# A stated order for TensorE: one attention layer of a later group at four fixed places of every gated step

## The chip, the cores and the metric

The kernel runs on one core of one Trainium2 chip. A core has TensorE (PE in the profile: matrix products and transposes, results in eight PSUM banks), VectorE (DVE), ScalarE (ACT), GpSimd (POOL), and SyncE (SP), whose queue issues the transfers. The metric is the device time of one execution in microseconds (us). Before the change it is 3129.03 us, the median of three runs (3125.44 to 3129.26).

## What is computed

128 graphs of 128 nodes with 256 features go through three attention layers and then a gated recurrent network of three steps. All is float32. Cut to what matters:

```python
# three attention layers, l = 0, 1, 2
h  = relu(layernorm(x))
Wh = h @ W                                    # per graph [128, 256]
e  = (Wh @ a1)[:, None] + (Wh @ a2)[None, :]  # [128, 128]
e  = where(e > 0, e, 0.2 * e)
p  = softmax(where(adj > 0, e, -9e15), axis=-1)
x  = x + elu(p @ Wh)                          # layer 2: (p @ Wh) * nodemask

# gated network, i = 0, 1, 2
h  = relu(layernorm(x))
for i in range(3):
    aggr = A.T @ (h @ weight[i])              # A = (adj != 0)
    r = sigmoid(aggr @ w_ih_r.T + b + h @ w_hh_r.T + b)
    z = sigmoid(aggr @ w_ih_z.T + b + h @ w_hh_z.T + b)
    n = tanh(aggr @ w_ih_n.T + b + r * (h @ w_hh_n.T + b))
    h = (1 - z) * n + z * h
x = x + h
```

The kernel computes `attention @ h` before the product with `W`, reads `Wh @ a1` and `Wh @ a2` as products of h with the vectors `W a1` and `W a2` (`VA`), and folds `weight[i]` into `w_ih` once at the start (`wc[i]`). The sigmoids are taken as tanh of half the argument.

## The kernel before

Graphs are worked on in 32 groups of four (G = 4, T = 512 columns). `gat(g)` is the three attention layers of a group, `gru(g)` its gated steps. PSUM has three pools of banks: "gat" 2, "gru" 4, "tr" 2. One layer:

```python
def attention(g, l, xt, cap):
    nm, rs = stats(xt, name)        # VectorE bn_stats/bn_aggr; GpSimd: rs = (var + eps) ** -0.5
    for b in range(G):              # ScalarE
        nc.scalar.activation(xn[:, b, :], xt[:, b, :], AF.Relu, bias=nm[:, b : b + 1])
    for b in range(G):              # VectorE: e[:, 0] = xn . VA[0]
        nc.vector.scalar_tensor_tensor(scr, xn[:, b, :], rs[...], VA[l][:, 0, :], ..., accum_out=e[:, 0, b : b + 1])
    nc.gpsimd.tensor_tensor(pr, xn, VA[l][:, 1 : 2, :]..., op=OP.mult)       # GpSimd
    for b in range(G):              # ScalarE: e[:, 1] = sum of pr
        nc.scalar.activation(pr[:, b, :], pr[:, b, :], AF.Copy, scale=rs[...], accum_out=e[:, 1, b : b + 1])
    yield
    for c in range(G):              # TensorE, "e" in the profile
        nc.tensor.transpose(e2[...], e[:, 1, c : c + 1].to_broadcast([P, P]), ident)
    # ... VectorE: em = min(e2 + e[:, 0], cap), leaky relu, row maximum nmx
    # ... ScalarE: pe = exp(em - max), sums;  VectorE: pe *= 1 / sum
    # ... GpSimd: xo = xt - 1
    yield
    for b in range(G):              # TensorE, "atp"
        nc.tensor.transpose(atp[...], pe[:, b, :], ident)
    # ... VectorE: at = atp * rs
    # ... TensorE "ahp": 2 x 4 products 128x128; copies ah by ScalarE and VectorE
    # ... TensorE "hp": 2 x 4 products 128x256; ScalarE t = exp(hp); VectorE: two xo per half
    yield xo
```

After the third layer the normalised features `hn` are turned by TensorE for the gated steps (`hTp`: eight transposes of 128x128, one copy on ScalarE, one on VectorE):

```python
hT = turned(hn, grp, "h0", f"{g}_3")
```

A gated step has 24 products of 128x512, eight of 128x128 (`agp`) and, from the second step on, eight transposes (`hnp`):

```python
for i in range(STEPS):
    for c in range(KD):                       # KD = 2
        nn, pr, pz = ...                      # three "gru" banks
        if c == 0: evac(0)                    # hnp transposes of h[0], ScalarE copy (not for i == 0)
        for k in range(KD):
            mm(nn, cn, whh, h, k, ...); mm(pr, cr, whh, h, k, ...); mm(pz, cz, whh, h, k, ...)
            if c == 0:
                aggregate(k)                  # agp: 4 products, VectorE copy ag[k]
                if k == 0: evac(1)
        # ScalarE: wn
        yield
        # TensorE r <- ag (k = 0, 1); ScalarE r = tanh; VectorE n = (r + 1) * wn
        # TensorE ni <- ag (k = 0, 1); VectorE n += ni; ScalarE n = tanh
        yield
        # TensorE z <- ag (k = 0, 1); ScalarE z = tanh
        # VectorE d = h[c] - n;  d = (z + 1) * d;  hnew[c] = 0.5 * d + n
        yield
# end: for k in 0, 1: hnp transposes of h[k]; VectorE o = hnp + xt; transfer out
```

The program emits whole streams, group after group:

```python
AHEAD = 2
for g in range(min(AHEAD, NG)):
    run(gat(g))
for g in range(NG):
    run(gru(g))
    if g + AHEAD < NG:
        run(gat(g + AHEAD))
```

What stands next to what on an engine is thus left to the scheduler of the language, which reorders the instructions of every engine by a model of their times when the program is built.

Of the kernel before, what the change touches and what calls it, by code (L numbers as in the profile page):

```python
# [8 lines left out]
FT = mybir.dt.float32  # L9
# [5 lines left out]
P = 128  # L15
# [6 lines left out]
def kernel(  # L22
# [23 lines left out]

    nc = tc.nc
# [3 lines left out]
    NG = B // G  # L51
    T = G * N
    STEPS = gweight.shape[0]
    assert N == P and B % G == 0 and B <= P and D == 2 * P and T == 512

    const = ctx.enter_context(tc.tile_pool(name="const", bufs=1))
    grp = ctx.enter_context(tc.tile_pool(name="grp", bufs=2))
    gw = ctx.enter_context(tc.tile_pool(name="gw", bufs=2))
    setup = ExitStack()
# [6 lines left out]

    def load(g):
        xt = grp.tile([P, G, D], FT, tag="x0", name=f"x_{g}")
        nc.sync.dma_start(xt, x[g * G : (g + 1) * G].rearrange("b n d -> n b d"))
        at = grp.tile([P, G, N], I32, tag="adj", name=f"adj_{g}")  # L70
        nc.sync.dma_start(at, adj[g * G : (g + 1) * G].rearrange("b i j -> i b j"))
        return xt, at

    loaded = {0: load(0)}


# [38 lines left out]

    def transposed(src, dst, nm_):
# [3 lines left out]
        for k in range(KD):  # L120
            for r0 in range(0, rows, 4):
                n = min(4, rows - r0)
                ps = bank("gat", f"{nm_}_{k}_{r0}")
                for r in range(n):
                    nc.tensor.transpose(
                        ps[:, r * P : (r + 1) * P], t[:, r0 + r, k * P : (k + 1) * P], ident
                    )
                nc.vector.tensor_copy(dst[:, k, r0 * P : (r0 + n) * P], ps[:, : n * P])
# [11 lines left out]
    for i in range(STEPS):  # L140
# [3 lines left out]
        for m in range(KD):  # L144
            for o0 in range(0, O3, 384):
                ps = bank("gat", f"wcp_{i}_{m}_{o0}")
# [18 lines left out]

    setup.close()
# [3 lines left out]
    def stats(xt, name):  # L170

        st = gw.tile([P, G, 6], FT, tag="st", name=f"st_{name}")
        mv = gw.tile([P, G, 2], FT, tag="mv", name=f"mv_{name}")
        for b in range(G):
            nc.vector.bn_stats(st[:, b, :], xt[:, b, :])  # L175
            nc.vector.bn_aggr(mv[:, b, :], st[:, b, :])  # L176
        nm = gw.tile([P, G], FT, tag="nm", name=f"nm_{name}")
        nc.vector.tensor_scalar(nm, mv[:, :, 0], -1.0, None, op0=OP.mult)
        ve = gw.tile([P, G], FT, tag="ve", name=f"ve_{name}")
        nc.gpsimd.tensor_scalar(ve, mv[:, :, 1], EPS, None, op0=OP.add)  # L180
        rs = gw.tile([P, G], FT, tag="rs", name=f"rs_{name}")
        nc.gpsimd.tensor_tensor(rs, ve, mhalf, op=OP.pow)  # L182
        return nm, rs

    def turned(v, pool, tag, name):

        hT = pool.tile([P, KD, T], FT, tag=tag, name=f"hT_{name}")
        for k in range(KD):
            ps = bank("gat", f"hTp_{name}_{k}")
            for b in range(G):  # L190
                nc.tensor.transpose(
                    ps[:, b * P : (b + 1) * P], v[:, b, k * P : (k + 1) * P], ident
                )
            if k % 2 == 0:
                nc.scalar.copy(hT[:, k, :], ps)
            else:
                nc.vector.tensor_copy(hT[:, k, :], ps)
        return hT

    def attention(g, l, xt, cap):  # L200

        name = f"{g}_{l}"
        nm, rs = stats(xt, name)

        xn = gw.tile([P, G, D], FT, tag="xn", name=f"xn_{name}")
        for b in range(G):
            nc.scalar.activation(xn[:, b, :], xt[:, b, :], AF.Relu, bias=nm[:, b : b + 1])  # L207

        e = gw.tile([P, 2, G], FT, tag="e", name=f"e_{name}")
        for b in range(G):  # L210
            scr = gw.tile([P, D], FT, tag="scr", name=f"scr_{name}_{b}")
            nc.vector.scalar_tensor_tensor(  # L212
                scr, xn[:, b, :], rs[:, b : b + 1], VA[l][:, 0, :], op0=OP.mult, op1=OP.mult,
                accum_out=e[:, 0, b : b + 1],
            )
        pr = gw.tile([P, G, D], FT, tag="pr", name=f"pr_{name}")
        nc.gpsimd.tensor_tensor(  # L217
            pr, xn, VA[l][:, 1 : 2, :].to_broadcast([P, G, D]), op=OP.mult
        )
        for b in range(G):  # L220
            nc.scalar.activation(  # L221
                pr[:, b, :], pr[:, b, :], AF.Copy, scale=rs[:, b : b + 1],
                accum_out=e[:, 1, b : b + 1],
            )
        yield

        e2 = bank("gat", f"e2_{name}")
        for c in range(G):
            nc.tensor.transpose(  # L229
                e2[:, c * P : (c + 1) * P], e[:, 1, c : c + 1].to_broadcast([P, P]), ident  # L230
            )

        em = gw.tile([P, G, N], FT, tag="em", name=f"em_{name}")
        for c in range(G):
            nc.vector.scalar_tensor_tensor(
                em[:, c, :], e2[:, c * P : (c + 1) * P], e[:, 0, c : c + 1], cap[:, c, :],
                op0=OP.add, op1=OP.min,
            )
        nc.vector.scalar_tensor_tensor(em, em, ALPHA, em, op0=OP.mult, op1=OP.max)
        nmx = gw.tile([P, G], FT, tag="nmx", name=f"nmx_{name}")  # L240
        nc.vector.tensor_reduce(nmx, em, axis=AX.X, op=OP.max, negate=True)  # L241
        pe = gw.tile([P, G, N], FT, tag="pe", name=f"pe_{name}")
        sm = gw.tile([P, G], FT, tag="sm", name=f"sm_{name}")
        for b in range(G):
            nc.scalar.activation(  # L245
                pe[:, b, :], em[:, b, :], AF.Exp, bias=nmx[:, b : b + 1], accum_out=sm[:, b : b + 1]
            )
        ri = gw.tile([P, G], FT, tag="ri", name=f"ri_{name}")
        nc.vector.reciprocal(ri, sm)
        if l == 2:  # L250
            nc.vector.tensor_mul(ri, ri, nmT[:, g * G : (g + 1) * G])
        nc.vector.tensor_tensor(
            pe, pe, ri.rearrange("p (g o) -> p g o", o=1).to_broadcast([P, G, N]), op=OP.mult
        )

        xo = grp.tile([P, G, D], FT, tag=f"x{l + 1}", name=f"xo_{name}", bufs=3 if l == 2 else 2)
        nc.gpsimd.tensor_scalar(xo, xt, 1.0, -1.0, op0=OP.mult, op1=OP.add)  # L257
        yield
        atp = bank("gat", f"atp_{name}")
        for b in range(G):  # L260
            nc.tensor.transpose(atp[:, b * P : (b + 1) * P], pe[:, b, :], ident)  # L261
        at = gw.tile([P, T], FT, tag="at", name=f"at_{name}")
        nc.vector.tensor_tensor(
            at.rearrange("p (g i) -> p g i", g=G), atp.rearrange("p (g i) -> p g i", g=G),
            rs.rearrange("p (g o) -> p g o", o=1).to_broadcast([P, G, N]), op=OP.mult,
        )

# [27 lines left out]
        yield xo  # L295

    done = {}

    def gat(g):
        xt, adj_t = loaded.pop(g)  # L300
        if g + 1 < NG:
# [168 lines left out]
```

## Time and profile before

| engine | busy us | share of the span |
|---|---|---|
| TensorE, products and transposes | 2941.1 | 94% |
| TensorE, weight loads (beside them) | 1714.3 | 55% |
| VectorE | 2163.8 | 69% |
| ScalarE | 1349.4 | 43% |
| GpSimd | 530.0 | 17% |

The span of the profiled execution is 3125.1 us. TensorE works in the first 50 us on setup (transposing and folding the weights), then on the first attention layers, and gated steps begin at 121 us. From 200 us on the picture repeats from group to group. A float32 product shows as two matmul records in the trace, a transpose as one. [...] the time of a product is read from the distance between starts. "Idle before" in brackets at the end of a timeline row is how long the engine had nothing running, and the arrow names what ended that.

### The profile page before, as it was taken

The page shows a single profiled execution, that of the slowest core. Times are in us where ns is not written, and L with a number is a line of the kernel's source. Part 1 is how long each engine was busy: PE and PEld are TensorE (multiplying, and loading weights), DVE is VectorE, ACT ScalarE, POOL GpSimd, SP SyncE. Part 2 cuts the span into 40 slices and gives each one's busy share as a digit, 9 for nine tenths or more (in the row PEclk, how much of TensorE's full clock was granted, in tenths as well). Part 3 has the DMA queues.
Part 4 walks back from the last instruction along what each step waited for, and adds up shares of the span by engine and source line. Part 5 has one row for each costly group of instructions (what it writes and reads, how often), then busy time and mean ns, then how long its engine had stood idle before and what let it go on. Part 6 is the DMA issues. An engine that isn't in the chain of part 4 may idle for free.

```text
span 3125.1 us, 32601 instructions
## 1 busy us (share of the span) xinstructions
PE 2941.1 (94%) x11105; PEld 1714.3 (55%) x11105; DVE 2163.8 (69%) x4731; ACT 1349.4 (43%) x3265; POOL 530.0 (17%) x454
## 2 busy tenths in 40 slices
PE   5699999999999999999999999999999999999999
PEld 3455555555555555555555555555555555555554
DVE  5667776767776777776777677677667677767663
ACT  1344444444444444444444444444444444444442
POOL 1212111212111212121112121112121121111110
PEclk8899999999999999999999999999999999999999
DMA  2000000000000000000000000000000000000000
GB/s 85 11 17 11 7 18 17 17 18 11 7 18 17 18 17 11 7 17 18 17 18 11 7 17 18 18 12 13 11 18 17 17 11 7 17 14 7 8 1 14
DMA packets 56199, 48.03 MB, mean 15 GB/s; under 512 B 3296, under 2 KB 55648, under 8 KB 56032
## 3 DMA queue, kind: packets, MB, share of 16 engines
q1 hardware_dynamic: 56032, 45.95, 4.6%
q8 instruction: 87, 1.43, 0.2%
q14 instruction: 80, 0.66, 0.1%
HBM read 29.17 MB, written 16.78 MB: 15 GB/s over the span
## 4 chain that ended last, share of the span: by engine, by line
PE 70%; DVE 13%; ACT 9%; POOL 6%; issue 1%; DMA 0%; ACTq 0%; SPq 0%; POOLq 0%; DVEq 0%
PE r L344 15%; PE z L344 15%; PE ni L344 9%; PE hp L285 7%; PE nn L344 7%; PE ahp L272 6%; POOL pr L217 5%; ACT xn L207 4%; PE agp L361 3%; DVE st L175 3%; DVE xo L294 3%; DVE xo L293 3%; ACT pr L221 2%; PE hnp L335 2%; PE e L229 2%; PE atp L261 2%
## 5 line engine op out<-in xcount | busy, mean ns | idle before, releaser
L212 DVE SCALAR_TENSOR_TENSOR scr<-xn,rs,va 128x256 f32<-128x256 f32 x384 | 386.0, 1053 | 73.0 <-POOL rs L182 71.1
L344 PE MATMUL r<-ag,wc 128*128 128x512 f32 x768 | 372.1, 593 | 0.0
L344 PE MATMUL ni<-ag,wc 128*128 128x512 f32 x768 | 371.4, 592 | 0.0
L285 PE MATMUL hp<-w,ah 128*128 128x256 f32 x1536 | 368.3, 383 | 0.7 <-DVE ah L279 0.7
L344 PE MATMUL z<-ag,wc 128*128 128x512 f32 x768 | 361.4, 592 | 0.0
L257 POOL TENSOR_SCALAR xo<-xo 128x1024 f32<-128x1024 f32 x64 | 67.5, 1055 | 1596.4 <-DVE mv L176 1596.4
L285 PEld LDWEIGHTS hp<-w,ah 128*128 128x128 f32 x1536 | 284.2, 190 | 76.8 <-DVE ah L279 26.3
L293 DVE SCALAR_TENSOR_TENSOR xo<-hp,xo 128x512 f32<-128x512 f32 x192 | 131.0, 683 | 253.6 <-ACT t L291 253.6
L221 ACT ACTIVATE pr<-pr,rs 128x256 f32<-128x256 f32 x384 | 190.4, 496 | 183.5 <-POOL pr L217 183.5
L291 ACT ACTIVATE t<-hp 128x512 f32<-128x512 f32 x192 | 114.7, 597 | 353.5 <-PE hp L285 353.5
L344 PE MATMUL nn<-h,whh 128*128 128x512 f32 x512 | 261.8, 593 | 0.0
L344 PE MATMUL z<-h,whh 128*128 128x512 f32 x512 | 261.5, 592 | 0.0
L344 PE MATMUL r<-h,whh 128*128 128x512 f32 x512 | 261.5, 592 | 0.0
L392 DVE SCALAR_TENSOR_TENSOR n<-r,wn 128x512 f32<-128x512 f32 x192 | 131.4, 685 | 185.2 <-ACT r L390 185.2
L217 POOL TENSOR_TENSOR pr<-xn,va 128x1024 f32<-128x1024 f32 x96 | 236.2, 2461 | 96.6 <-ACT xn L207 96.6
L245 ACT ACTIVATE pe<-em,nmx 128x128 f32<-128x128 f32 x384 | 148.8, 389 | 209.3 <-DVE nmx L241 209.3
L361 PEld LDWEIGHTS agp<-am,hn 128*128 128x128 f32 x1536 | 204.5, 192 | 61.3 <-issue 61.0
L344 PEld LDWEIGHTS z<-ag,wc 128*128 128x128 f32 x768 | 143.3, 190 | 167.5 <-issue 167.4
L397 ACT ACTIVATE n<-n,bi 128x512 f32<-128x512 f32 x192 | 138.3, 720 | 213.1 <-DVE n L396 210.5
L390 ACT ACTIVATE r<-r,brz 128x512 f32<-128x512 f32 x192 | 131.3, 684 | 215.1 <-PE r L344 215.0
L344 PEld LDWEIGHTS ni<-ag,wc 128*128 128x128 f32 x768 | 143.5, 190 | 142.7 <-issue 132.2
L361 PE MATMUL agp<-am,hn 128*128 128x128 f32 x1536 | 218.2, 275 | 0.0
(91 smaller groups left out, 4636.6 us busy)
## 6 DMA issues: line engine op xcount, KB each, us to landing
x<-in_x_dram SPq DMA_DIRECT2D x32, 512.0 KB, 3.9
out_dram<-o SPq DMA_DIRECT2D x32, 512.0 KB, 2.9
adj<-in_adj_dram SPq DMA_DIRECT2D x32, 256.0 KB, 2.7
w<-in_L_gnn_W_dram SPq DMA_DIRECT2D x3, 256.0 KB, 6.9
ab<-in_L_gnn_a_dram SPq DMA_DIRECT2D x3, 256.0 KB, 6.6
whh_ld<-in_L_gnn_w_hh_dram SPq DMA_DIRECT2D x1, 768.0 KB, 8.4
wih_ld<-in_L_gnn_w_ih_dram SPq DMA_DIRECT2D x1, 768.0 KB, 5.9
gt_ld<-in_L_gnn_weight_dram SPq DMA_DIRECT2D x3, 256.0 KB, 2.6
```

Source lines behind the costliest of these rows:

```text
L212: nc.vector.scalar_tensor_tensor(scr, xn[:, b, :], rs[:, b : b + 1], VA[l][:, 0, :], op0=OP.mult, op1=OP.mult, accum_out=e[:, 0, b : b + 1],)
L217: nc.gpsimd.tensor_tensor(pr, xn, VA[l][:, 1 : 2, :].to_broadcast([P, G, D]), op=OP.mult)
L221: nc.scalar.activation(pr[:, b, :], pr[:, b, :], AF.Copy, scale=rs[:, b : b + 1], accum_out=e[:, 1, b : b + 1],)
L245: nc.scalar.activation(pe[:, b, :], em[:, b, :], AF.Exp, bias=nmx[:, b : b + 1], accum_out=sm[:, b : b + 1])
L272: nc.tensor.matmul(ps[:, c * P : (c + 1) * P], xn[:, c, k * P : (k + 1) * P], at[:, c * P : (c + 1) * P], start=True, stop=True,)
L285: nc.tensor.matmul(hp[:, b * D : (b + 1) * D], ah[:, k, c * P : (c + 1) * P], W[l][:, k, :], start=(k == 0), stop=(k == KD - 1),)
L293: nc.vector.scalar_tensor_tensor(u, hp, 0.0, u, op0=OP.max, op1=OP.add)
L344: nc.tensor.matmul(ps, w[:, k, c * P : (c + 1) * P], v[k], start=start, stop=stop)
L361: nc.tensor.matmul(ps[:, b * P : (b + 1) * P], hn[k][b], am[:, b, :], start=True, stop=True)
L390: nc.scalar.activation(r, pr, AF.Tanh, bias=brz[:, cr : cr + 1], scale=0.5)
L392: nc.vector.scalar_tensor_tensor(n, r, 1.0, wn, op0=OP.add, op1=OP.mult)
L397: nc.scalar.activation(n, n, AF.Tanh, bias=bi[:, cn : cn + 1])
```

## The change

The change states TensorE's order in the program and alters what is needed for it. All other engines are still ordered by the scheduler. What it does:

- `manual_schedule` for TensorE around the main loop: its instructions stay as the program emits them. The gated steps are emitted with a raised priority for the other engines.
- Every gated step has four places. At each, one piece of an attention layer of a later group is emitted: e, then atp, then the ah products, then the hp products (with the next layer's statistics, xn, scr and pr). Step 0 of group g carries layer 2 of group g+1, step 1 layer 1 of group g+2, step 2 layer 0 of group g+3. The first statistics of group g+3 are emitted at the end of step 1.
- The groups are 2, then 31 times 4, then 2 graphs, so that the first chain and the last group are shorter.
- hTp is gone: VectorE transposes 32x32 blocks, and a round trip through device memory (one transfer out, four in) puts the blocks in place. Step 0 reads h with a strided view.
- The setup of the gated weights is emitted among the first attention layers; inputs are loaded two groups ahead.

It is for a TensorE that always has a product ready: gated products between the pieces give the other engines time to prepare the next piece. The core of the diff, cut:

```diff
+    SIZES = [2] + [G] * ((B - 4) // G) + [2]
+    URGENT = 300
 ...
-        hT = turned(hn, grp, "h0", f"{g}_3")
+            nc.vector.transpose(
+                tr.rearrange("p j (k b c) -> p k b j c", k=KD, b=n)[:, k],
+                hn[:, :, k * P : (k + 1) * P].rearrange("p b (j r) -> p b j r", j=Q),
+            )
+        nc.sync.dma_start(d.rearrange("q r j f -> (q r) j f"), tr)
+        for j in range(Q):
+            nc.sync.dma_start(
+                hT[j * 32 : (j + 1) * 32], d[:, :, j, :].rearrange("q r f -> r q f")
+            )
 ...          # gru, one step: the four places are the yields
+                    if c == 0:
+                        aggregate(k)
+                        if k == 0:
+                            yield
+                            evac(1)
 ...
+            evac(0)
+            for c in range(KD):
+                wn, pr, pz = yield from h_parts(c)     # nn, r, z of h; agp; wn
+                if c == 1:
+                    yield
+                # r <- ag; r = tanh; n
+                if c == 1:
+                    yield
+                # ni <- ag; n; z <- ag; z = tanh; d; h
+                if c == 0:
+                    yield
 ...
-    for g in range(NG):
-        run(gru(g))
-        if g + AHEAD < NG:
-            run(gat(g + AHEAD))
+    with tc.manual_schedule(engines={mybir.EngineType.PE}):
+        for g in range(NG):
+            work = gru(g)
+            for i in range(STEPS):
+                for p in range(4):
+                    with tc.high_priority(offset=URGENT):
+                        next(work)
+                    piece(g + 1 + i)
+                if i == 1:
+                    piece(g + 3)
+            with tc.high_priority(offset=URGENT):
+                next(work)
```

Two details matter for the order. The ni and z products of the second half (c = 1) come after the fourth place, so they are emitted with the next step's first part. And after step 2 they are followed at once by the group's last transposes and its output, then by the next group's step 0.

## The prediction

> **What bounds the kernel now.** I read the page first (busy shares, slices), then TensorE's list of waits, then the timeline of one middle group.
>
> ```profile
> PE 2941.1 (94%) x11105; PEld 1714.3 (55%) x11105; DVE 2163.8 (69%) x4731; ACT 1349.4 (43%) x3265; POOL 530.0 (17%) x454
> ...
> PEclk8899999999999999999999999999999999999999
> ```
>
> ```profile
> PE e L229 <- ACT pr L221: 102.4, 125, 8.4
> PE hTp L191 <- ACT hn L317: 29.1, 33, 6.1
> PE atp L261 <- DVE pe L252: 16.6, 3, 5.8
> ```
>
> TensorE is busy 94% of the time and its clock is granted in full from the third of the forty slices on. The waits are few: total us, count, longest. The work itself can be counted. In the timeline a 512-column product is two rows of one matmul and starts 0.86 us after the one before; a 128x256 one takes 0.43, a 128x128 one 0.22, a transpose 0.108. One group of four graphs needs 72 x 0.858 = 61.8 (gated steps), 24 x 0.22 = 5.3 (aggregation), 24 x 0.22 = 5.3 and 24 x 0.43 = 10.3 (attention), 48 transposes = 5.2 and 8 more for hTp = 0.9: 88.8 us. In the trace the same place of two groups is 94.27 us apart (hp at 231.56, 325.82, 420.10 in the chain). So about 5.5 us of each group are gaps, most of them the wait of e for pr. The start adds to that: the first gated product runs at 121 us, and TensorE is busy only 51 of the first 100 us.
>
> The second thing to read is how long a layer's row of engines takes from its last product (hp, ending at 1554.15) to the next layer's e:
>
> ```profile
> 1554.15 1.02 PE L344 MATMUL ni<-ag,wc 128*128 128x512 f32 x2
> ...
> 1554.35 0.60 ACT L291 ACTIVATE t<-hp 128x512 f32<-128x512 f32 x1 [1.13 <-PE hp L285]
> ...
> 1556.04 0.67 DVE L294 SCALAR_TENSOR_TENSOR xo<-t,xo 128x512 f32<-128x512 f32 x1
> ...
> 1559.12 1.71 ACT L207 ACTIVATE xn<-xo,nm 128x256 f32<-128x256 f32 x4 [0.84 <-DVE nm L178]
> ...
> 1560.90 2.45 POOL L217 TENSOR_TENSOR pr<-xn,va 128x1024 f32<-128x1024 f32 x1 [0.28 <-ACT xn L207]
> ...
> 1561.07 2.56 DVE L212 SCALAR_TENSOR_TENSOR scr<-xn,rs,va 128x256 f32<-128x256 f32 x1
> ...
> 1563.39 0.51 ACT L221 ACTIVATE pr<-pr,rs 128x256 f32<-128x256 f32 x1 [1.99 <-POOL pr L217]
> ...
> 1564.04 0.32 PE L229 MATMUL e<-ident,e 128*128 128x128 f32 x1 [1.14 <-ACT pr L221]
> ```
>
> Columns: start, length, engine, line, what. From hp's end to xn 4.97 us, from xn to ACT's pr 4.27, the four pr with their accumulator reads 2.08 (until 1565.47): 11.3 us. This chain is the quantity the change plays with.
>
> [...] the scr row above takes 2.56 us beside pr instead of its median 0.482. [...]
>
> ```profile
> 118.28 2.17 PE L191 MATMUL hTp<-ident,hn 128*128 128x128 f32 x8 [6.05 <-ACT hn L317]
> 120.24 1.06 PE L361 MATMUL agp<-am,hn 128*128 128x128 f32 x4
> 121.09 1.18 PE L344 MATMUL nn<-hT,whh 128*128 128x512 f32 x2
> ```
>
> After 6.05 us idle the eight transposes take 1.96 us start to start instead of 0.87, the next row 0.85 instead of 0.44: about 1.7 us lost in all. [...]
>
> **The change, part by part.**
>
> 1. hTp goes: 0.9 us of TensorE per group, about 28 in all, with two copies. In come two block transposes on VectorE (estimate 0.6 to 0.7 each, as its other one-pass 128x512 operations of 0.68) and five transfers. Those are issued two gated steps (about 60 us) before they are needed, against 2 to 4 us each: hidden.
>
> 2. Group sizes 2, 4 x 31, 2. The same columns in all. The first chain before the gated steps is half as wide and no longer shares the start with a whole second group. I estimate gated steps from about 80 us (before: 121).
>
> 3. The order. TensorE's order in a middle group is now fixed, and the instruction order of the changed kernel, which can be read without running it, shows what the others do. In step 2 of each group TensorE comes to e of layer 0 of group g+3. Between that and the hp of step 1 (layer 1 of group g+2) lie only ni and z (4 x 0.858 = 3.43), hnp 0.43, three products 2.57 and agp 0.89: 7.3 us. ScalarE's order there, in 29 of the 33 groups, is:
>
> ```
> z_1_1  hn_2_0  xn_2 x4  pr_2 x4  xn_0 x4  pr_0 x4  hn_2_1
> ```
>
> xn_2 and pr_2 belong to the layer that follows that hp, xn_0 and pr_0 to layer 0, which TensorE waits for. So the chain above runs first, then a second one behind it. Counted from hp's end: xn_2 starts at 4.97 plus what VectorE's order now puts in front (d 0.6 and the first x statistics 0.4) = 6.0; pr_2 done on ScalarE at 6.0 + 4.3 + 2.1 = 12.4; [...] then come the rest of the x statistics, so xn_0 starts at about 12.6; pr_0 is done at 12.6 + 4.3 + 2.1 = 19.0, e at 19.3. Without a wait e would end at 7.3 + 0.43 = 7.75. **Wait: 11.5 us in each of 29 groups.** It is long enough to halve the clock: 2.0 more.
>
> 4. The group's end. hnp of the second half of h now follows the last z with only the first hnp (0.43) between. The end of the kernel before shows what that costs:
>
> ```profile
> 3117.01 0.60 PE L335 MATMUL hnp<-ident,h 128*128 128x128 f32 x4
> ...
> 3118.97 0.69 DVE L408 SCALAR_TENSOR_TENSOR h<-d,n 128x512 f32<-128x512 f32 x1
> ...
> 3119.81 0.63 PE L335 MATMUL hnp<-ident,h 128*128 128x128 f32 x4 [2.19 <-DVE h L408]
> ```
>
> 2.19 us there with VectorE free; with hp's xo and statistics in VectorE's queue I count 2.7, in every group. Before, the next group's products stood in this gap.
>
> 5. r takes ag of the second half 0.86 us after agp ends; the copy needs 0.68 and VectorE's queue has reduce or em in front: 0.3 to 0.5 per step, estimate 0.9 per group (in step 2 hidden behind the cold clock). The other places hold: atp is needed 9 us after e, its chain takes 5 to 6; ah 5 us after atp, needs 0.7; hnp in a step 4.3 us after z, needs 2.3.
>
> **Sum.** A middle group: 88.0 + 11.5 + 2.0 + 2.7 + 0.9 = 105.1 us (before 94.27). Start 80. First group of two graphs, with three whole layers between its short steps: 35 + 18.3 of work and about 27 of waits (e of layer 0 alone 15.5) = 80. Middle groups 29 x 105.1 = 3048. Group 30 has no layer 0 beside it, group 31 only half a layer: 83 and 76. Last group of two and the output: 46. Together 80 + 80 + 3048 + 83 + 76 + 46 = 3413. I predict **3410 us**, 9% slower.
>
> **Rivals.** A: the stated order does what it is for. All waits fall: 32 x 88.0 = 2816, start 80, end 15, about 2910. For it speak the room between a layer's other places and the long slack of layers 1 and 2 (a step and more). Against it speaks the count of part 3: two chains of 6.4 us behind one of 6.0 do not fit into 7.3. B: ScalarE has room (43% busy) and layer 0's xn is done before the other layer's pr, so e waits only 3 to 5 us and the clock stays up: 88 + 4 + 3.6 = 95.6 per group, total near 3130, no change. The order read from the program speaks against it[...]. C: VectorE (67 of 94 us busy before) becomes the bound: it would need 88 us of work per group and has about 68; it only delays.
>
> **Range and chances.** The wait of part 3 is certain in sign; its size is the sum of about ten rows and may be off by 2 us (60 in all), the clock by 1.5 per group (45), the start by 25. Range 3300 to 3490. Faster by over 2%: 0.04 (A, if I read a dependence wrongly). Within 2%: 0.04 (B). Slower: 0.92.
>
> **What would show it.** TensorE's waits would be led by e for ScalarE's pr: some 30 times 11 us, 330 in all, in step 2 only; hnp for h about 2.7 x 33 = 85; TensorE's busy share near 85%; granted clock below full in every slice. The same place of two groups would be 105 us apart; gated steps begin near 80. Wrong if e's wait is under 5 us, if the clock stays full, or if the strided operand of step 0 (blocks of 32) makes its products slower than 0.858.

## The result, and the profile after

| | us | ratio to before, 95% interval |
|---|---|---|
| before | 3128.6 | 1 |
| after | 3568.0 | 1.1406 [1.1387, 1.1426] |
| predicted | 3410 (3300 to 3490) | |

The change makes the kernel 14% slower. It went the way the prediction described, but 158 us further than the 3410 us forecast. The page of the changed kernel, its busy time and two of its lines of forty slices, first:

```profile
PE 3040.0 (85%) x10993; PEld 1773.1 (50%) x10993; DVE 2200.4 (62%) x4830; ACT 1347.5 (38%) x3264; POOL 558.4 (16%) x468
...
PE   5578889888889888889888898888898888898899
...
PEclk8789999999999999999999999999999999999999
```

TensorE has fewer instructions than before (10993 against 11105: 256 of hTp are gone, and one group more brings 144) and yet is busy 99 us longer, in the main because of its clock. A 9 in the row of the clock means 0.9 or more; the mean over the whole span is 0.927, against 0.991 before, and by windows it is below 1.00 in all slices but the 39th. Its waits (total us, times, longest):

```profile
PE e L175 <- ACT pr L165: 332.8, 36, 19.9
PE hnp L306 <- DVE h L386: 88.6, 34, 3.4
PE r L315 <- DVE ag L336: 48.4, 52, 1.5
PE atp L203 <- DVE em L197: 19.6, 4, 10.2
```

Of the 332.8 us, 289 are 29 waits at e of layer 0, one a group, of which 26 are 10.05 to 10.07 us long. Here is one of them in the timeline (start, length, engine, line, what, and idle time with its releaser):

```profile
1590.01 1.88 PE L315 MATMUL ni<-ag,wc 128*128 128x512 f32 x4
...
1595.85 1.71 ACT L153 ACTIVATE xn<-xo,nm 128x256 f32<-128x256 f32 x4 [0.75 <-DVE nm L138]
...
1600.13 0.51 ACT L165 ACTIVATE pr<-pr,rs 128x256 f32<-128x256 f32 x1 [2.57 <-POOL pr L157]
...
1601.41 0.71 DVE L135 BATCH_NORM_STATS2 st<-x 128x6 f32<-128x256 f32 x2
...
1602.57 1.70 ACT L153 ACTIVATE xn<-x,nm 128x256 f32<-128x256 f32 x4 [0.37 <-DVE nm L138]
...
1606.91 0.51 ACT L165 ACTIVATE pr<-pr,rs 128x256 f32<-128x256 f32 x1 [2.63 <-POOL pr L157]
...
1607.57 1.95 PE L175 MATMUL e<-ident,e 128*128 128x128 f32 x4 [10.06 <-ACT pr L165]
1609.31 1.06 PE L306 MATMUL hnp<-ident,h 128*128 128x128 f32 x4
1610.16 1.53 PE L315 MATMUL nn<-h,whh 128*128 128x512 f32 x2
```

hp of the other layer ends at 1590.01, where ni starts. Its chain (first xn and pr) runs before layer 0's own (the xn made from x, and the second pr), and e ends, where hnp starts, at 1609.31, 19.3 us after hp. The e transposes then take 1.74 us from start to start instead of 0.43. The granted clock is 0.50 there (1607.57 to 1611.00), but that alone would make them 0.85, as it does with the four of hnp behind them. The rest is waiting: each of the four needs its own row of pr from ScalarE, and these rows come 0.49 us apart. The weight loads (PEld) of the transposes show it:

```profile
1608.06 0.18 PEld L175 LDWEIGHTS e<-ident,e 128*128 128x128 f32 x1 [0.31 <-ACT pr L165]
1608.55 0.18 PEld L175 LDWEIGHTS e<-ident,e 128*128 128x128 f32 x1 [0.31 <-ACT pr L165]
```

The same stretch in numbers, from the answer by windows (window, its us, then busy us and instruction counts of TensorE, its weight loads, VectorE, ScalarE and GpSimd, the granted clock, DMA). It covers 29 middle groups, between two equal places:

```profile
233.34:3361.64 3128.30, 2711.53 (x9722) 1555.61 (x9722) 1960.60 (x4250) 1210.62 (x2920) 502.27 (x407) 0.93 0.07 22
```

Divided by 29, a group takes 107.87 us: 93.50 busy and 14.37 idle. The best kernel below, without a wait in such a stretch, is busy 88.39 us for the same group. The 5.1 us between 93.50 and 88.39 are TensorE at work more slowly than at the full rate. Added up over the rows whose next one starts late, it is 3.2 us a group from e on, 1.4 after the wait of hnp and 0.2 after r's, 4.8 in all. Of the 3.2, 1.3 are e itself, which waits for pr row by row and shows as busy; so the half clock is 3.5 us a group.

### The profile page after: what moved, and what is told of

It reads as the page before. It is cut to its first block, busy times and chain, and to the rows that moved or that the text cites. A ratio compares the mean times of both kernels' runs of the same rounds, so it can differ in the third digit from the quotient of the medians.

```text
span 3566.3 us, 33209 instructions
## 1 busy us (share of the span) xinstructions
PE 3040.0 (85%) x10993; PEld 1773.1 (50%) x10993; DVE 2200.4 (62%) x4830; ACT 1347.5 (38%) x3264; POOL 558.4 (16%) x468
## 4 chain that ended last, share of the span: by engine, by line
PE 56%; DVE 23%; ACT 8%; POOL 7%; issue 5%; DMA 0%; ACTq 0%; SPq 0%; POOLq 0%; DVEq 0%
PE r L315 16%; PE z L315 11%; PE nn L315 8%; PE ahp L215 5%; PE hp L229 5%; PE ni L315 5%; DVE xo L238 3%; DVE xo L237 3%; DVE st L135 3%; POOL pr L157 3%; POOL rs L142 2%; DVE scr L160 2%; PE e L175 2%; ACT hn L261 2%; PE agp L332 2%
## 5 line engine op out<-in xcount | busy, mean ns | idle before, releaser
L315 PE MATMUL nn<-h,whh 128*128 128x512 f32 (+1 forms) x792 | 436.6, 636 | 0.0
L315 PE MATMUL r<-h,whh 128*128 128x512 f32 (+1 forms) x792 | 429.3, 626 | 0.0
L315 PE MATMUL r<-ag,wc 128*128 128x512 f32 (+1 forms) x792 | 385.9, 593 | 48.9 <-DVE ag L336 48.4
L315 PE MATMUL z<-h,whh 128*128 128x512 f32 (+1 forms) x792 | 407.7, 597 | 0.0
L175 PE MATMUL e<-ident,e 128*128 128x128 f32 x384 | 99.2, 339 | 334.4 <-ACT pr L165 332.8
L315 PE MATMUL z<-ag,wc 128*128 128x512 f32 (+1 forms) x792 | 361.9, 579 | 0.0
L315 PE MATMUL ni<-ag,wc 128*128 128x512 f32 (+1 forms) x792 | 361.9, 579 | 0.0
L376 ACT ACTIVATE n<-n,bi 128x512 f32<-128x512 f32 (+1 forms) x198 | 140.5, 709 | 401.3 <-DVE mv L136 214.6
L315 PEld LDWEIGHTS r<-h,whh 128*128 128x128 f32 x792 | 165.1, 208 | 204.5 <-issue 178.0
L315 PEld LDWEIGHTS z<-h,whh 128*128 128x128 f32 x792 | 161.7, 204 | 199.2 <-issue 182.9
L157 POOL TENSOR_TENSOR pr<-xn,va 128x1024 f32<-128x1024 f32 (+1 forms) x99 | 234.5, 2369 | 75.8 <-ACT xn L153 69.4
```

Of the source, the lines that this page charges most:

```text
L157: nc.gpsimd.tensor_tensor(pr, xn, VA[l][:, 1:2, :].to_broadcast([P, n, D]), op=OP.mult)
L175: nc.tensor.transpose(e2[:, b * P : (b + 1) * P], e[:, 1, b : b + 1].to_broadcast([P, P]), ident)
L315: nc.tensor.matmul(like(ps, v[k]), w[:, k, c * P : (c + 1) * P], v[k], start=start, stop=stop)
L376: nc.scalar.activation(n, n, AF.Tanh, bias=bi[:, cn : cn + 1])
```

## The experiments

All of them are edits of the changed kernel, and each ratio is to the kernel before. The first four take up one term of the prediction each, or the order itself.

**Layer 0 earlier.** Its first part (loads, statistics, xn, scores) is emitted behind step 0 and not behind step 1. This needs a third buffer for `rs` and `xn`.

```diff
-                if i == 1:
+                if i == 0:
                     piece(g + 3)
```

> Only layer 0's first piece (statistics, xn, scr, pr of group g+3) is emitted a step earlier, at the end of step 0 instead of step 1, with three buffers for xn and rs. TensorE's order is untouched. Theory (e of layer 0 waits because its xn and pr stand behind those of the other layer on ScalarE): the wait of e for pr falls from 333 us to under 60, the cold clock after it goes, so 29 x (11.6 + 0.9) = 360 us less: about 3205 us, with the waits of hnp (89) and r (48) still there or a little larger. Rival (ScalarE, GpSimd and VectorE have no room for the chain anywhere between the urgent gated operations, so the wait only moves to atp or ag): above 3400 us, with atp or r waits grown by over 150 us.

Measured: 3314.3 us, ratio 1.0587 [1.0569, 1.0606]. This is the largest single gain, 254 us, but it falls between the two expectations, because VectorE's copies now stand behind layer 0's work:

```profile
PE r L315 <- DVE ag L336: 126.5, 72, 3.1
...
PE e L175 <- ACT pr L165: 29.0, 6, 19.9
PE agp L332 <- DVE ag L336: 24.1, 29, 1.3
```

e's wait went from 332.8 to 29.0, all of it in the first groups. r's wait rose from 48.4 to 126.5, and the aggregation has a new one. Its timeline shows where that comes from:

```profile
1561.65 2.63 DVE L160 SCALAR_TENSOR_TENSOR scr<-xn,rs,va 128x256 f32<-128x256 f32 x1
...
1564.47 0.67 DVE L336 COPY ag<-agp 128x512 f32<-128x512 f32 x1
...
1565.20 1.13 PE L315 MATMUL r<-ag,wc 128*128 128x512 f32 x2 [2.83 <-DVE ag L336]
```

One of the four score products on VectorE takes 2.63 us instead of 0.48, and the copy that TensorE waits for is behind it, with one short piece of em between. In the changed kernel such a product lies beside GpSimd's: scr takes 2.55 us from 1604.61, pr runs from 1604.36 to 1606.88. Over all 384 score products the mean is 1.035 us in this run; in the run with all three edits and without GpSimd's product (below) it is 0.481 over 768. Why the one is long beside GpSimd's was not shown.

**Output turned later.** Both turns of the output (hnp) are moved behind the next group's first products and its first aggregation.

```diff
+        yield
         o = tile_of(rw, n_g, [D], "o", f"o_{g}", bufs=1)
 ...                  # in the loop, behind the next group's first next(work)
+                        if last is not None:
+                            next(last)
+                            last = None
```

> Only the group's last transposes and output are moved behind the next group's first three products and agp (2.57 + 0.89 us of ready work). Theory (hnp waits 2.9 us per group for h because only 0.43 us lie between z and it, and this wait also halves the clock in about half the groups): hnp's wait falls from 89 us to under 10, 31 x 2.9 + 31 x 0.8 = 115 us less: about 3455 us. Rival (given back: in the groups that start cold, r of step 0 does not wait for ag, in the warm ones it waits 1.7 us, so half of the gain returns as ag wait): about 3510 us, with r's wait for ag grown from 48 to 80 us or more.

Measured: 3638.9 us, ratio 1.1631 [1.1613, 1.1648]: slower than the changed kernel, outside both expectations. hnp's second turn takes the bank of the first aggregation, and that bank is free only when VectorE has copied it:

```profile
1562.67 2.55 DVE L160 SCALAR_TENSOR_TENSOR scr<-xn,rs,va 128x256 f32<-128x256 f32 x1
...
1566.73 0.68 DVE L336 COPY ag<-agp 128x512 f32<-128x512 f32 x1
...
1567.47 1.12 PE L306 MATMUL hnp<-ident,h 128*128 128x128 f32 x4 [5.21 <-DVE ag L336]
```

A wait of 2.7 us became one of 5.2. The move put a new dependence, through a bank, behind the same VectorE queue. In the changed kernel the clock was halved behind the old wait in 24 of 28 groups, not in half of them as the theory had it.

**First half of ag first.** In the first half of a step z and ni take ag[0] before r takes ag[1].

```diff
+                if c == 0:
+                    ni = bank("gru", f"ni_{name}_{c}")[:, :TG]
+                    mm(pz, cz, wc[i], ag, 0, False, False)
+                    mm(ni, cn, wc[i], ag, 0, True, False)
                 for k in range(KD):
                     mm(pr, cr, wc[i], ag, k, False, k == KD - 1)
 ...                  # ni and z then start at k = 1 - c
```

> Only the order of the first half's gated products is changed: z and ni of the first ag half stand before r, so that 1.72 us more lie between the last agp and the first product that needs the second ag half. Theory (r waits because VectorE's copy of ag has other work in front): r's wait for ag falls from 48 us to under 8: about 3520 us. Rival (the copy is late by a whole queue, 3 us and more, or r's later tanh delays z's bank and h): within 15 us of 3568.

Measured: 3492.2 us, ratio 1.1163 [1.1144, 1.1181]. r's wait of 48.4 us is gone and no other replaces it. The gain of 76 us is larger than the wait: TensorE's busy time also fell by 27.5 us (3040.0 to 3012.5). Less half clock is a part of that, since the granted clock rose from 0.927 to 0.931; how large a part was not measured.

**No stated order.** Everything of the change stays, but `manual_schedule` goes, and the scheduler orders TensorE as in the kernel before.

```diff
-    with tc.manual_schedule(engines={mybir.EngineType.PE}):
+    if True:
```

> The changed kernel with TensorE's order left to the scheduler again; all else (sizes 2, 4 x 31, 2, block transposes and round trip, emission and priorities) stays. Theory (the stated order is the whole cost, the other parts are free or a gain): at or below the kernel before, 2980 to 3140 us, e's wait for pr near 100 us. Rival (the other parts cost: strided step 0, block transposes in VectorE's queue, the urgent priorities, late x statistics): above 3250 us.

Measured: 4344.0 us, ratio 1.3885 [1.3864, 1.3906]. The theory falls. The rival's number is passed by far, but none of the parts that it names is shown to cost this. TensorE's three longest waits:

```profile
PE atp L203 <- DVE em L197: 420.9, 63, 13.0
PE agp L332 <- ACT hn L261: 192.9, 33, 8.8
PE hnp L306 <- DVE ri L194: 100.6, 28, 3.6
```

With this emission the scheduler runs the attention layers as blocks; in the group at 1610 us two of the three have no gated product between e and atp. So stating an order is not in itself what costs: left free, the same emission is slower by 776 us. That the places cost is shown by the runs that move them. This run doesn't say what a free order would do with another emission; that wasn't tried.

**Only the second turn later.** hnp_3_1 alone goes behind the next group's three products, ahead of the aggregation whose bank stood in the way before.

```diff
+                    if i == 0 and c == 0 and k == 0 and late:
+                        next(late.pop())       # the output's second turn
                     if c == 0:
                         aggregate(k)
 ...                  # the output, ahead of its second turn
+            if k == 1:
+                yield
```

> Only the second turn of the output, hnp_3_1, is put behind the next group's first three products and ahead of its first aggregation, where VectorE's copy of an aggregation cannot stand in its way. Theory: the wait of 2.7 to 3.0 us at each group's end is TensorE having nothing else ordered, and the half clock that follows in some groups comes from it. Then the waits put down to h fall from 88.6 us to under 10, the few us of half clock after a group's end go too, and the time is 3568 - 88 - 20 = about 3460 (3445 to 3485). Rival: the three products only bring the next wait nearer (the first product that needs an ag), so the 88 us turn up there, and the time stays over 3530. The waits of layer 0's e are 333 us either way.

Measured: 3542.7 us, ratio 1.1329 [1.1312, 1.1346]. The wait for h fell from 88.6 to 4.2, but r's wait for ag rose from 48.4 to 116.7, as the rival said. Only 25 us are gained. Some 6 us after the moved turn, which starts at 1528.20, TensorE stands still again, and VectorE sets the time anyway:

```profile
1536.36 0.69 DVE L336 COPY ag<-agp 128x512 f32<-128x512 f32 x1
...
1537.10 1.22 PE L315 MATMUL r<-ag,wc 128*128 128x512 f32 x2 [2.58 <-DVE ag L336]
```

**Layer 0 earlier and first half of ag first** (the first and the third edit).

> The early layer 0 (alone 3314 us, with 126.5 us of r waiting for ag and 24.1 us of the second aggregation waiting for an ag) together with the products of ag's first half ahead of those of its second. Theory: the two are independent, and the reordering takes away the whole of r's wait as it did alone: 3314 - 126 = about 3190 (3170 to 3215), with the 24 us of the aggregation and the 88 us at the groups' ends left. Rival: VectorE is late by more than one product covers once layer 0's work lies in front of its copies, so that what is taken from r is given back at the next aggregation; then the time is 3240 or more.

Measured: 3204.3 us, ratio 1.0244 [1.0229, 1.0259], inside the theory's range. r's waits fell from 126.5 to 32.5, while atp's for em rose from 31.7 to 67.7.

**All three.**

> All three: early layer 0, first half of ag first, last turn behind the next group's first products. Theory: what is left is the work of a group, 88.0 us, plus the aggregation's waits: 3190 - 88 - 20 = about 3080 (3060 to 3110), under the 3129 of the kernel before. Rival: once TensorE no longer stands still for the others, VectorE's queue is the next bound, and waits for an ag or for em come up in place of the ones removed: 3140 or more.

Measured: 3152.9 us, ratio 1.0079 [1.0063, 1.0096]. The rival holds: atp waits 86.6 us for em and r 54.4 us for ag. A wait of VectorE's making came up in place of each one removed.

**The start.** The three layers of group 0 stand ahead of all else.

```diff
-    first_group(5)
-    piece(1)
-    layer(1)
-    first_group(4)
+    first_group(13)
 ...                  # behind the weights
-    layer(1)
-    first_group(4)
+    piece(1)
+    layer(1)
+    layer(1)
     piece(2)
     layer(2)
```

> Only the start is changed: the three layers of group 0 stand ahead of all else in the program, and the layers of groups 1 and 2 that are needed before the loop come after the weights. Theory: the first gated step began at 119.65 us and not near 80 because group 0's chain shared VectorE, ScalarE and GpSimd with groups 1 and 2 and the weights; alone its three layers take about 19 us each, its h lands before 85 us and the first gated step begins by 90 us; at most half of the 30 us is then lost again in the first group, which waits for group 1's layers: 3568 - 15 to 30 = 3538 to 3553. Rival: the layers of groups 1 and 2 only come later, the first group waits for all of it, and the time is 3560 or more.

Measured: 3579.5 us, ratio 1.1445 [1.1428, 1.1462]; the rival holds. Its timeline:

```profile
79.15 1.19 PE L315 MATMUL nn<-h,whh 128*128 128x256 f32 x2 [0.29 <-DMA h<-d]
...
245.71 0.44 PE L306 MATMUL hnp<-ident,h 128*128 128x128 f32 x2 [3.36 <-DVE h L386]
```

The first gated product starts at 79.15 instead of 119.65, but the layers of groups 1 and 2 come later, and the first group ends at 245.7 instead of 233.3. The start and the first group are one stretch of chains; moving the gated products inside it gains nothing.

**ScalarE copies the second aggregation**, in the changed kernel.

```diff
-                nc.vector.tensor_copy(t, ps)
+                (nc.scalar.copy if k == 1 else nc.vector.tensor_copy)(t, ps)
```

> The changed kernel with one edit: ScalarE instead of VectorE copies each step's second aggregation out of PSUM. Theory: the wait of r for ag, 48 us where 30 were reckoned, is VectorE's queue: the copy stands behind the scores' products, one of which takes 2.6 us and not 0.5 while GpSimd's product runs, and ScalarE is waiting for that same GpSimd product and free. Then r's waits for VectorE's ag fall from 48.4 us to under 10, no wait for ScalarE's takes their place, and the time is 3568 - 40 to 50 = 3520 to 3530. Rival: ScalarE's queue is no freer (the relu of an attention layer's input, 1.7 to 2.1 us, stands there), the wait is put down to ScalarE's copy with 40 us or more, and the time stays within 10 us of 3568.

Measured: 3503.9 us, ratio 1.1199 [1.118, 1.1218]. r's waits fell from 48.4 to 2.4 and TensorE's busy time by 17 us. The theory holds, and the gain, 64 us, is larger than expected by the fall in busy time; the granted clock rose from 0.927 to 0.929, so less half clock is again a part of it.

**The same copy, with all three edits.**

> The same edit in the kernel with all three changes (3152.9 us). Theory: its waits of r for ag (54.4 us) go, and VectorE, with 0.69 us a step less to do, is in time with em in most steps (86.6 us of atp waiting for em, of which some 28 belong to the first groups): 3153 - 54 - 20 to 40 = 3060 to 3080, under the 3129 of before. Rival: the order on VectorE is one long queue, and the wait only moves from r to atp a few us later in the same step: 3120 or more.

Measured: 3223.0 us, ratio 1.0305 [1.0289, 1.0320]: 70 us slower than without it. The rival holds. In one step of a group the scheduler now puts ScalarE's r between the exponentials, and VectorE's n, which waits for r, ahead of the reciprocal; em comes late:

```profile
1533.63 0.69 DVE L378 SCALAR_TENSOR_TENSOR n<-r,wn 128x512 f32<-128x512 f32 x1 [1.90 <-ACT r L376]
...
1535.86 1.09 PE L203 MATMUL atp<-ident,em 128*128 128x128 f32 x4 [3.47 <-DVE em L197]
```

So an edit that helped alone hurts beside others, since every other engine's order is made anew.

**Scores on VectorE alone, with all three edits.** GpSimd's product and ScalarE's four sums go; VectorE makes both halves of e.

```diff
-        nc.gpsimd.tensor_tensor(pr, xn, VA[l][:, 1:2, :].to_broadcast([P, n, D]), op=OP.mult)
+        for s in (1, 0):
             for b in range(n):
                 nc.vector.scalar_tensor_tensor(
-                    scr, xn[:, b, :], rs[:, b : b + 1], VA[l][:, 0, :], ...
-                    accum_out=e[:, 0, b : b + 1])
-        for b in range(n):
-            nc.scalar.activation(pr[:, b, :], pr[:, b, :], AF.Copy, ..., accum_out=e[:, 1, b : b + 1])
+                    scr, xn[:, b, :], rs[:, b : b + 1], VA[l][:, s, :], ...
+                    accum_out=e[:, s, b : b + 1])
```

> The kernel with all three changes, with GpSimd and ScalarE taken out of the scores: the second half of e is made like the first, by four more products with a sum on VectorE (0.48 us each), so GpSimd's product of 2.35 us and ScalarE's four sums are gone. Theory: GpSimd's product is what makes VectorE's products long (one of four takes 2.6 us instead of 0.5), so four more of them cost VectorE 4 times 0.57 = 2.3 us and give back 2.1, the copies of ag come sooner or at the same time, e comes sooner, and the time is 3153 or less, down to 3090. Rival: VectorE is the bound wherever a copy waits, eight products in a row of 0.57 us stand ahead of the copy, and the time grows to over 3180.

Measured: 3153.5 us, ratio 1.0081 [1.0066, 1.0096], the same as without it. But the waits are no longer spread: r's and the aggregation's (54.4 and 24.0) are gone, and one is left that grew from 86.6:

```profile
PE atp L197 <- DVE em L191: 155.8, 62, 10.3
```

VectorE's busy time even fell (2167.6 to 2127.1 us): the 768 products took 330.3 us (0.481 each), where 384 had taken 364.7 (0.992 each) in the run with GpSimd's product.

**Both edits, with all three.**

> Both edits in the kernel with all three changes. Theory: [...] without either r's and the aggregation's waits fall under 20 us together and the time is near the work of a group, 88 us: 3030 to 3070. Rival: VectorE's larger work makes atp wait longer for em, and the time is above that of the copy on ScalarE alone.

Measured: 3150.9 us, ratio 1.0072 [1.0057, 1.0087]. Neither number was met. The wait is at atp again, now 127.5 us in 56 places, 2.3 each. The profile puts it down to ScalarE's n, but em, which atp reads, is done no earlier: at 1559.28 us in one group, n at 1559.31.

Three loads of VectorE and ScalarE, one time, one place: this pointed at the place. From e to atp TensorE has 7.7 us of products (9 x 0.858), one hnp and one agp, 9.0 us in all; the chain from the start of e to the end of em took 11.3 us (the median, here as in the run before).

**atp behind three more products**, with the three edits and the scores on VectorE.

```diff
+                    elif k == 0:               # second half of the step, behind nn, r, z of h[0]
+                        yield
 ...
                 hnew.append(hc)
-                if c == 0:
-                    yield
```

> The three changes and the second half of e made by VectorE (3153.5 us, with 155.8 us of atp waiting for em in 62 places, about 2.2 us each beyond the first groups), and the place of atp moved behind the first three of the second half's products. Theory: the place is 2 us too early for the chain from e to em, three products are 2.57 us, and the wait goes but for the 20 to 30 us of the first groups: 3153 - 125 = about 3025 (3010 to 3045), for the first time under the 3129 of before. Rival: VectorE is the bound, and the time comes back as waits of ahp for at or of r for ag: 3090 or more.

Measured: 2978.8 us, ratio 0.9522 [0.9506, 0.9538]. It is below the range expected: atp's waits fell from 155.8 to 24.2 us in four places, all in the first groups, and no wait came up elsewhere.

**The same place, with the scores left on GpSimd and ScalarE.**

> The three changes (3152.9 us: atp for em 86.6, r for ag 54.4, the aggregation for ag 24.0) and the later place of atp, with the scores on GpSimd and ScalarE as in the kernel before. Theory: only the 60 us of atp go, r's and the aggregation's waits stay: 3085 to 3100. Rival: with TensorE earlier by as much, the copies of ag are later by as much in its count, and the time is 3120 or more.

Measured: 3123.6 us, ratio 0.9985 [0.9979, 0.9992]. atp's waits fell from 86.6 to 27.7, but r's 54.3 and the aggregation's 24.0 stayed as they were and new ones of ahp (11.7) and z (7.2) came up; the number is the rival's. The lighter chain and the later place are both needed.

**The same place, with both edits.**

> As the first of these, with ScalarE copying the second aggregation (3150.9 us with atp at its old place, 127.5 us of atp's waits put down to ScalarE's n). Theory of the place: 3010 to 3045 here too, within 15 us of the first, because neither engine's copy is then waited for. Rival: ScalarE's copy stands behind or ahead of something that matters, and the two differ by over 20 us.

Measured: 2971.9 us, ratio 0.9501 [0.9487, 0.9515], the fastest kernel, 5% under before. It is below the range expected, and within 15 us of its sister, as the theory of the place said. Its page, and one middle group by windows:

```profile
PE 2883.1 (97%) x10993; PEld 1719.8 (58%) x10993; DVE 2070.2 (70%) x5499; ACT 1188.8 (40%) x2595; POOL 322.4 (11%) x369
...
PEclk8799999999999999999999999999999999999999
```

```profile
1543.90:1632.43 88.53, 88.39 (x338) 51.94 (x337) 63.66 (x169) 36.84 (x81) 10.01 (x11) 1.00 0.09 27
```

TensorE is busy 88.39 of 88.53 us at full clock. The same 10993 instructions took it 3040.0 us in the changed kernel and 2883.1 here; most of these 157 us are the 4.8 us in each of 29 groups, 139 in all: 3.5 of half clock and 1.3 of e waiting row by row.

**Scores on VectorE, in the changed kernel alone**, to part the length of the chain from the place.

> The changed kernel with the second half of e made by VectorE and nothing else: layer 0's first part stays behind step 1. Theory of the place: the statistics of layer 0 stand on VectorE behind layer 2's scores (in the changed kernel until 1601.31 us, 11.3 us after hp), which take no less time with eight products of 0.49 us than with four of which one is held; only the last piece, from xn to e, gets shorter, by some 2.5 us of the 10: e's waits 333 to between 230 and 270, time 3480 to 3510. Rival: the chain over GpSimd and ScalarE is what is long, e's waits fall below 130 us, and the time is 3430 or less.

Measured: 3437.9 us, ratio 1.0988 [1.097, 1.1006], between the two expectations:

```profile
PE e L169 <- DVE scr L159: 215.3, 35, 14.4
```

The shorter chain takes 118 of 333 us from e's wait, more than the 2.5 us a group that I reckoned.

**Layer 0 put back, in the best kernel.**

> The best kernel (2971.9 us) with layer 0's first part put back behind step 1. Theory of the place: e waits some 7.5 us in each of 29 groups, and TensorE is at half clock for about 2 us of loss after it: 2972 + 29 * 9.5 = about 3245 (3200 to 3270), over the 3129 of before. Rival: with the other edits in, VectorE is free in time for layer 0, and the time stays under 3100.

Measured: 3234.8 us, ratio 1.0338 [1.0323, 1.0354], as the theory said. e's waits are back at 215.4 us, the value of the run before, and busy time is up by 78 us (2961.4). One place of one piece is worth 263 us.

## Why the prediction fell short

Direction and mechanism held; the size did not. Against the sum of 3413 us, 155 are missing, in the steps that failed. The start and the first group were reckoned at 80 us each as if group 0 had the engines to itself, and took 119.65 and 113.7. In the middle groups the wait of hnp was counted without the half clock behind it (1.4 us a group), and r's wait for ag at half its size (0.9 for 1.7). What follows the 29 groups, 83 + 76 + 46 = 205 us, took 204.7 (3566.3 less 3361.64). Point by point, by the prediction's own parts:

1. *hTp and the transfers.* Held. The two block transposes took 0.69 us each (62 of them), and TensorE never waited for h's transfer (2.7 us from issue to landing, median).
2. *Start at 80 us.* Failed: 119.65, 40 us more. The first chain was taken to be alone. In the changed kernel it shares VectorE, ScalarE and GpSimd with layers of groups 1 and 2:

```profile
93.15 5.39 PE L229 MATMUL hp<-w,ah 128*128 128x256 f32 x24
...
118.40 1.46 PE L175 MATMUL e<-ident,e 128*128 128x128 f32 x3 [19.86 <-ACT pr L165]
119.65 1.14 PE L315 MATMUL nn<-h,whh 128*128 128x256 f32 x2
```

The 24 hp records at 93.15 are eight of group 0, which has two graphs, and sixteen of a group of four, side by side. The run with group 0 alone started at 79.15, so the chain itself was reckoned rightly, but it then ended the first group later. *First group 80* failed with it: 113.7 (119.65 to 233.34), 34 more. The two terms were added as if independent, though the layers of groups 1 and 2 have to be done before either ends.

3. *Layer 0's e.* The wait held: 19.3 us from hp to the end of e as predicted, 10.06 idle plus 1.31 in e, which waits for the other rows of pr, where 11.5 was the sum. *2.0 us of half clock* held too, as a mean: 3.2 a group with e's 1.3 in it, so 1.9 behind it, but from 1.1 to 2.8 in single groups. One detail was incomplete: xn of layer 0 was last held up not by ScalarE's pr but by VectorE's statistics (0.37 us for nm), which stand behind the other layer's scores, one of which took 2.55 us (from 1597.83) beside GpSimd's pr (1597.63 to 1600.09).

4. *The group's end.* The wait of 2.7 us held: 2.71 in nearly every group, 88.6 in all against 85. The term failed all the same, since half clock followed the wait in 24 of 28 groups, 1.4 us a group that the sum does not have.

5. *r for ag.* 0.9 us a group was too small: 48.4 us over 29 groups is 1.7. The reason was right: of the waits, 31 with 36.0 us in all come with the row-maximum reduce (nmx) right in front of the copy. Only the size was off, 1.2 us each where 0.3 to 0.5 were reckoned:

```profile
1676.15 1.31 DVE L268 STREAM_TRANSPOSE tr<-hn 128x512 f32<-128x512 f32 x2 [1.28 <-ACT hn L261]
...
1679.23 0.69 DVE L187 TENSOR_REDUCE nmx<-em 128x4 f32<-128x512 f32 x1
1679.83 0.68 DVE L336 COPY ag<-agp 128x512 f32<-128x512 f32 x1
...
1680.57 1.13 PE L315 MATMUL r<-ag,wc 128*128 128x512 f32 x2 [1.23 <-DVE ag L336]
```

In this step the two new block transposes, 1.31 us, stand in the same queue, and the reckoning left them out of it. That they make the wait longer is argued from the order alone; no run takes them away.

The same part said that the chain to atp takes 5 to 6 us of the 9 after e. From the start of e to the end of em it took 7.8 in the changed kernel (median), which other waits hid; without them it became the last bound.

A middle group was to take 105.1 and took 107.87, 2.8 more, 80 us over 29 groups: 1.4 from the half clock at the group's end, 0.8 from r for ag, and the rest, some 0.6, mostly from the work itself (88.53 in the best kernel where 88.0 was counted). The largest term, layer 0's e, was right, and so were the signs named for it: 333 us of waits (330), TensorE 85% busy, one slice alone at full clock. The strided operand of step 0 costs nothing: nn of the step that begins at 1639.79 starts 0.86 us before r. With 40 us of the start and 34 of the first group that is 154 us, the miss.

Of the rivals, A (all waits fall, 88.0 us a group) described what the stated order can do once its places fit: 88.53 in the best kernel. B is refuted by the 10.06 us. C, VectorE as the bound, is refuted as a bound of throughput, since the best kernel keeps VectorE at 70%; it was true of VectorE's order, whose copies or em held TensorE in several of the runs above.

What stays open: what the new group sizes, the block transposes with their transfers and the raised priority cost or give, since no run takes one of them back alone; why the scheduler orders the other engines as it does in each case, and how far a better start could go; the best kernel still has its first gated product at 113 us.

## What to carry to other kernels

When one engine's order is fixed in the program, each place is a deadline for another engine's chain: count, from the instruction order, the work between the two places and the length of the chain, and move the place by one set of products where it does not fit; here layer 0's place alone was worth 263 us of the best kernel's 2972. Take waits away together and look again at where they come up: of eight edits made alone, five gave 25 to 254 us and three made it slower, while the place of atp gave 29 us on top of the first three and 175 with the scores on VectorE as well. A wait on TensorE like those of 2.71 to 2.99 us here is to be reckoned with the half clock that can follow it (1.3 to 1.7 us in 24 of 28 places), and a start with everything that shares its engines.

## What the runs showed of the hardware that was not expected

A wait of 2.7 us, and even one of 2.40 (at 3361.64), was followed by a granted clock of 0.50, in most places and not in all. At the end of two groups of the changed kernel:

```profile
1531.69 0.66 PE L306 MATMUL hnp<-ident,h 128*128 128x128 f32 x4 [2.99 <-DVE h L386]
1532.18 1.42 PE L315 MATMUL nn<-h,whh 128*128 128x512 f32 x2
1533.40 1.92 PE L315 MATMUL r<-h,whh 128*128 128x512 f32 x2
...
1639.29 0.66 PE L306 MATMUL hnp<-ident,h 128*128 128x128 f32 x4 [2.71 <-DVE h L386]
1639.79 1.02 PE L315 MATMUL nn<-h,whh 128*128 128x512 f32 x2
1640.65 1.02 PE L315 MATMUL r<-h,whh 128*128 128x512 f32 x2
```

In the first, the two records of r take 1.92 us, in the second 1.02. Over 28 middle groups with a wait of 2.71 to 2.99 us there, the four rows from hnp to z lost 1.3 to 1.7 us in 24 and nothing in four, so it is not the length alone that decides. By the clock records of the changed kernel's trace all 66 stretches at half clock begin on one grid of 3.413 us, and the two waits fall on it differently. Here are the window in which most of the first wait lies and the next one, then the two windows between which the second wait is split (window, its us, then as above; the granted clock is the third number from the end):

```profile
1529.26:1532.68 3.42, 0.99 (x6) 0.76 (x7) 2.45 (x6) 1.17 (x4) 1.51 (x2) 1.00 0.00 0
1532.68:1536.09 3.41, 3.41 (x6) 1.35 (x5) 3.19 (x4) 0.95 (x4) 2.61 (x3) 0.50 0.34 113
1635.08:1638.49 3.41, 1.50 (x7) 0.69 (x5) 3.37 (x10) 1.30 (x2) 1.04 (x1) 1.00 0.00 0
1638.49:1641.90 3.41, 2.61 (x9) 1.45 (x10) 2.22 (x8) 1.70 (x4) 2.41 (x3) 1.00 0.00 0
```

The first wait leaves TensorE 0.99 busy us in one window, and the next window runs at 0.50. The second is split between two windows with 1.50 and 2.61 busy us, and the clock stays at 1.00. From 200 us on, the windows of the grid at full clock sort without an exception: after 56 with up to 1.39 busy us the clock was halved, after 799 with 1.42 or more it was not. So in this trace some 2.0 us without work in one window (3.41 less 1.4) went with half clock in the next. Other kernels and shapes were not measured for it, and what makes the grid was not shown.
